# A transformer block conditioned by adaptive norms: the first block loaded and normalized in finer pieces, the last quarter's way through DRAM in two halves, and a new order

## The chip, the cores and the metric

The kernel runs on one NeuronCore of a Trainium2 chip. The core has five engines with their own instruction streams: TensorE (matrix products, PE in the profile, its weight loads PEld), VectorE (DVE), ScalarE (ACT), GpSimd (POOL) and SyncE (SP), whose stream here only issues transfers; some transfers are issued on ACT's stream. The metric is the device time of one execution in microseconds (us), median of several runs.

## The reference

All data are float32. `x` is [2, 2048, 512], `cond` [2, 512]; the weights are `ada_w` [512, 3072], two 512 x 512 matrices `ssm_w1`, `ssm_w2`, and `ff_w1` [512, 1024], `ff_w2` [1024, 512].

```python
emb = silu(t) @ ada_w + ada_b
shift_msa, scale_msa, gate_msa, shift_mlp, scale_mlp, gate_mlp = split(emb, 6)
norm = _ln(x) * (1.0 + scale_msa[:, None]) + shift_msa[:, None]
h = gelu(norm @ ssm_w1 + ssm_b1, approximate=False)
x = x + gate_msa[:, None] * (h @ ssm_w2 + ssm_b2)
norm2 = _ln(x) * (1.0 + scale_mlp[:, None]) + shift_mlp[:, None]
hf = gelu(norm2 @ ff_w1 + ff_b1, approximate=True)
x = x + gate_mlp[:, None] * (hf @ ff_w2 + ff_b2)
```

`_ln` subtracts the mean of a row and divides by the root of its variance plus 1e-6.

## The kernel before

The 4096 tokens are eight blocks of 512. A block lies with 128 partitions and four slots (`C = 4`): a partition holds four tokens of 512 features. Products of two matrices are done with seven smaller products instead of eight (`P1` to `P7`, on quarters and on sums of quarters of the operands); the sums are tensor_tensor instructions on VectorE or POOL (`tt`, line 345). In the feed-forward part this is done twice, so that a product has 49 leaves.

**Start.** `small_loads` brings the condition, `ada_b` and the biases as rows; TensorE turns them into columns (`turn_by_pe`, line 393) and VectorE copies them to `cols_t` (line 1405). `load_x(0, 2)` brings the first block in two pieces of two slots. `load_ada(g)` brings the sixth `g` of `ada_w`: 0 the shift, 1 the scale (in two pieces by rows). `w1` comes in two pieces by rows. Until the first data are there TensorE multiplies the identity with itself (`warm`). `normed_half(h)` takes statistics of slots 2h and 2h+1 (lines 613, 614), computes the root on POOL (646, 647) and the scale factors on VectorE (649 to 652), and normalizes one slot on VectorE (672) and one on ACT (363). `rows_of` multiplies silu(cond) with a sixth of `ada_w`, 32 columns of the array at a time; `modulation` then transposes the result in 32 x 32 pieces on VectorE (570), adds `ada_b` (573) and so makes `mods[g]`. `turn_in(h)` transposes the normalized half on TensorE, `turn_out(h)` scales and shifts it into `turned` (747 on VectorE, 363 on ACT). Then the products of the first block begin (`ssm1`, line 383), in the order P1, P2, P5 (`FRESH`): P1 and P2 take the first half of `w1`'s columns, P5 the sum of the two quarters of the second half, done on POOL.

**Middle.** The state-space part goes over the blocks, the feed-forward part over four pairs of blocks: `up` and `down`, whose leaves TensorE does one after the other while VectorE adds them up.

**End.** `down` of the last pair gives four quarters (two halves of the features for each of two blocks). Two of them go back to token order through DRAM (`quarter_out`): VectorE transposes in 32 x 32 pieces (1160), four transfers write `back_d`, others read it back, an add joins the rest `x1` (1177) and the result goes out. The other two are turned on TensorE (`turned_by_pe`): a scaled add (1136) of each leaf, two transposes, an add (1288), and the output.

**Order.** A class `Plan` collects all operations with a cost and with the operations that each depends on. `order` simulates the engines and puts the operations of each in a line; the list `MOVED` then takes single operations out and puts them behind a named one on a named engine ("v" VectorE, "a" ACT, "g" POOL, "s" SP), and `BEHIND` makes an operation wait for another. TensorE's operations stay in program order. The numbers in both lists count the operations in the order in which the program adds them. Transfers take turns at eight semaphores, so one is issued when the one eight before it has landed.

Of the kernel before, what the change touches and what calls it, by code (L numbers as in the profile page):

```python
# [58 lines left out]
)  # L59


# [226 lines left out]
def kernel(  # L288
# [21 lines left out]
    C = 4  # L310
# [1227 lines left out]
```

## Time and profile before

| what | value |
|---|---|
| median of 3 runs | 560.1 us (560.06 to 560.17) |
| profiled execution | 560.02 us, span 558.2 us |
| TensorE busy | 552.0 us (99% of the span), 2809 products |
| VectorE busy | 475.3 us (85%) |
| POOL busy | 384.0 us (69%) |
| ACT busy | 282.3 us (51%) |
| transfers | 123.68 MB, mean 222 GB/s |

The profile gives one execution. A row of a timeline has the start, the duration, the engine, the line, the operation with output and input tiles, how many instructions were merged, and in brackets how long the engine was idle before and what ended it. A float32 product shows as two records. Lines 345, 363, 372, 383, 393 and 405 are helpers that all stages use.

### The profile page before, as it was taken

The numbers are of one execution on the slowest core, as the hardware profiler recorded it, in microseconds if no ns is written. First come the engines' busy times: TensorE is split into PE (matmuls) and PEld (weight loads), VectorE is DVE, ScalarE is ACT, GpSimd is POOL, SyncE is SP. The second block draws the span as 40 slices with busy tenths as digits, with TensorE's granted clock in tenths as the row PEclk, the third lists the DMA queues.
The fourth block names the chain that finished last, engine by engine and source line by source line (L and its number), as shares of the span: only waits on it lengthen the run. The fifth ranks groups of instructions, "written<-read, shape, count | busy, mean of one in ns | idle before, by whom it ended". The sixth has DMA issues, their size and how long they took to land.

```text
span 558.2 us, 8726 instructions
## 1 busy us (share of the span) xinstructions
PE 552.0 (99%) x2809; PEld 482.0 (86%) x2809; DVE 475.3 (85%) x857; ACT 282.3 (51%) x523; POOL 384.0 (69%) x466
## 2 busy tenths in 40 slices
PE   8999999999999999999999999999999999999996
PEld 4888889899898988888888888888888888888885
DVE  5796878989778579799999987789988889898887
ACT  3473957675787845656305347414346414344230
POOL 2788639988855279985766868676757777539762
PEclk9999999999999999999999999999999999999999
DMA  8964699988399987995101999711998712983426
GB/s 311 399 234 115 193 354 275 360 260 267 113 292 323 290 318 231 329 300 188 40 37 38 285 305 323 229 39 42 293 322 286 234 39 59 326 285 112 153 76 188
DMA packets 66945, 123.68 MB, mean 222 GB/s; under 512 B 5668, under 2 KB 34260, under 8 KB 65364
## 3 DMA queue, kind: packets, MB, share of 16 engines
q1 hardware_dynamic: 64880, 121.80, 66.4%
q10 hardware_dynamic: 2020, 1.34, 0.8%
q8 instruction: 22, 0.36, 0.3%
q14 instruction: 23, 0.19, 0.1%
HBM read 77.89 MB, written 44.18 MB: 219 GB/s over the span
## 4 chain that ended last, share of the span: by engine, by line
PE 97%; DMA 2%; DVE 1%; DVEq 0%; issue 0%
PE bank L383 96%; DMA fw<-in_L_cond_ada_w_dram 1%; PE bank L393 1%; DMA fw<-in_L_cond_ada_b_dram 0%; DVE hidden L345 0%; DVE near L345 0%; DVE turned L747 0%; DVE rows L1136 0%; DVE bank L570 0%; DVEq L1533 0%; DVE mod L573 0%
## 5 line engine op out<-in xcount | busy, mean ns | idle before, releaser
L383 PE MATMUL bank<-turned,ring 128*128 128x256 f32 x896 | 210.1, 380 | 0.2 <-DVE turned L747 0.2
L383 PEld LDWEIGHTS bank<-turned,ring 128*128 128x128 f32 x896 | 167.9, 190 | 23.0 <-ACT turned L363 0.5
L345 DVE TENSOR_TENSOR hidden<-bank,hidden 128x512 f32<-128x512 f32 (+2 forms) x178 | 126.6, 739 | 22.2 <-PE bank L383 19.6
L383 PE MATMUL bank<-near,hidden 128*128 128x256 f32 (+1 forms) x470 | 95.0, 349 | 0.0
L383 PEld LDWEIGHTS bank<-near,hidden 128*128 128x128 f32 x470 | 82.2, 190 | 9.1
L383 PE MATMUL bank<-far,fw 128*128 128x256 f32 (+1 forms) x354 | 85.8, 374 | 0.0
L345 POOL TENSOR_TENSOR turned<-turned 128x512 f32<-128x512 f32 (+1 forms) x58 | 66.7, 1162 | 24.7 <-DVE turned L345 10.8
L383 PE MATMUL bank<-ring 128*128 128x256 f32 x336 | 82.3, 379 | 0.0
L345 DVE TENSOR_TENSOR rows<-bank,rows 128x256 f32<-128x256 f32 (+1 forms) x142 | 66.0, 479 | 15.4 <-PE bank L383 13.4
L383 PEld LDWEIGHTS bank<-far,fw 128*128 128x128 f32 x354 | 66.6, 190 | 8.7
L383 PEld LDWEIGHTS bank<-ring 128*128 128x128 f32 x336 | 63.7, 190 | 9.0 <-issue 0.3
L372 ACT COPY bank<-bank 128x512 f32<-128x512 f32 (+2 forms) x84 | 37.8, 449 | 62.5 <-PE bank L383 59.1
L363 ACT ACTIVATE hidden<-hidden,cols 128x512 f32<-128x512 f32 (+1 forms) x66 | 44.9, 710 | 42.0 <-DVE hidden L345 41.9
L345 POOL TENSOR_TENSOR hidden<-hidden 128x128 f32<-128x128 f32 (+2 forms) x44 | 45.0, 1033 | 26.0 <-DVE hidden L345 10.8
L383 PE MATMUL bank<-near,fw 128*128 128x256 f32 (+1 forms) x246 | 60.6, 376 | 0.0
L383 PE MATMUL bank<-hidden,fw 128*128 128x256 f32 (+1 forms) x216 | 53.3, 376 | 0.0
L383 PEld LDWEIGHTS bank<-near,fw 128*128 128x128 f32 x246 | 46.4, 190 | 6.1
L363 ACT ACTIVATE turned<-turned,mod,mod 128x512 f32<-128x512 f32 x56 | 42.3, 806 | 10.3 <-DMA turned<-turned 10.3
L383 PEld LDWEIGHTS bank<-hidden,fw 128*128 128x128 f32 x216 | 40.3, 190 | 5.9 <-issue 0.4
L345 POOL TENSOR_TENSOR ring<-turned,ring 128x256 f32<-128x256 f32 x41 | 29.6, 733 | 22.0 <-PE bank L383 19.0
L363 ACT ACTIVATE rows<-rows,gb,mod 128x512 f32<-128x512 f32 (+1 forms) x34 | 26.3, 787 | 33.2 <-DVE rows L345 21.3
L345 POOL TENSOR_TENSOR fw<-fw 128x256 f32<-128x256 f32 (+1 forms) x36 | 34.5, 968 | 7.0 <-DVE far L345 2.6
(123 smaller groups left out, 736.2 us busy)
## 6 DMA issues: line engine op xcount, KB each, us to landing
ring<-fw_parts SPq DMA_DIRECT2D x28, 512.0 KB
turned<-far SPq DMA_DIRECT2D x52, 256.0 KB
ring<-fw_parts SPq DMA_DIRECT2D x28, 384.0 KB
turned<-turned SPq DMA_DIRECT2D x32, 256.0 KB
back<-far SPq DMA_DIRECT2D x52, 128.0 KB
rows<-back SPq DMA_DIRECT2D x13, 512.0 KB
fw_parts<-fw SPq DMA_DIRECT2D x21, 256.0 KB
fw<-in_L_cond_ada_w_dram SPq DMA_DIRECT2D x5, 1024.0 KB
```

Of the source, the lines that this page charges most:

```text
L345: lambda E: E.tensor_tensor(o, a, b, f),
L363: lambda E: E.activation(o, a, func, bias=bias, scale=scale),
L372: plan.add("a", lambda E: E.copy(o, a), [o], [a], {"a": cost}, {"a": cost + 60})
L383: lambda E: E.matmul(o, lhsT, rhs, start=start, stop=stop, skip_group_check=True, **kw),
L393: lambda E: E.matmul(o, a, identity, start=start, stop=stop, is_transpose=True, skip_group_check=True),
```

## The change

- A row of ones and `ada_b`'s scale part (`one_more`) and a tile of ones (`two`) are set; `begin_rows` adds scale bias plus one to the scale's rows as the first TensorE product of their accumulation. The transposed rows are then used in place (`scale_t`), and VectorE adds nothing for g = 1. Two `warm` products behind the turn of the small rows fall away.
- The first block is loaded as slot 0, slot 1, slots 2 and 3; the scale's sixth in pieces of two, one and one row blocks; `w1` in two pieces by columns.
- TensorE does `turn_in(0)` ahead of both `rows_of`, slot by slot.
- The last quarter through DRAM (`by_half`) is written, read back, added and put out in two halves of its features. The first such quarter's adds are all on VectorE in the last pair.
- The last leaf (P4) of the last quarter is scaled, added and put out in two pieces.
- `MOVED` has 239 entries instead of 158, `BEHIND` 66 instead of 86; all entries are new. Among them: `(2, "a", 21)` puts the load of `ada_b`'s rows behind the first Silu on ACT, `(0, "g", -1)` and `(20, "g", 0)` put the memsets of `one_more` and `two` first on POOL, `(45, "v", 41)` puts the copy of the small columns behind the third of the four small VectorE steps, `(131, "s", 13)` and `(132, "s", 131)` put two loads of the gate's bias behind the scale's second piece, `(47, "a", 120)` puts an early Gelu (which loads its table) behind `turn_out(1)`.

```diff
+    one_more, two = kb(hidden_r, 30, 2)[:2], kb(hidden_r, 29, 1)[:2, P : P + G]
+    scale_t = kept("scale", P)
+    mods[1] = cut(scale_t, "p (n q) -> p n q", n=KD)[:, :, :B]
...
-    def rows_of(g, bank, midway=lambda: None):
+    def rows_of(g, bank, begun=False):
...
-            if k == KD // 2:
-                midway()
             for m in range(M):
-                mm(pa[m * G : (m + 1) * G, :P], silu[:, k, :], w[:, k, m], k == 0, k == KD - 1, (0, m * G))
+                mm(pa[m * G : (m + 1) * G, :P], silu[:, k, :], w[:, k, m], k == 0 and not begun, k == KD - 1, (0, m * G))
...
+    def begin_rows(bank):
+        for m in range(M):
+            o, row = banks[bank][m * G : (m + 1) * G, :P], cut(one_more, "p (n m q) -> p m n q", n=KD, q=G)[:, m]
+            mm(o, two, row, True, False, (0, m * G))
+
+    def modulation(g, bank, begun=False):
+        pa = rows_of(g, bank, begun)
+        o, a = scale_t if begun else pa[:, P : 2 * P], pa[:, :P]
         plan.add("v", lambda E: E.transpose(o, a), [o], [a], {"v": 210}, {"v": 290})
+        if begun:
+            return
...
+        closing = s + 1 == NBLK // 2
+        by_half = closing and blk == 1
+        band = cut(bands[n], "p (e a c r) -> p e c a r" if by_half else "p (a c e r) -> p e c a r", a=M, c=C, e=2)
...
+            if by_half:
+                half = kb(bands[n], 2 * e, 2)
+                for f in range(M):
+                    dma(halves[e, :, :, f].rearrange("a q r -> q a r"), cut(half[f * G : (f + 1) * G], "p (a r) -> p a r", a=M), queue(f) if e else "s")
+                dma(kb(flat, 2 * e, 2), halves[e].rearrange("a q f r -> (a q) (f r)"))
+        x, to = rest_in(s, d, blk, rest[n])
+        if by_half:
+            for e in range(2):
...
+                tt("vg", o, a, o, ALU.add)
+                dma(to[:, :, c], x[:, :, c], "s")
...
-                scaled_add(r1, t, columns(s, 1, e, 0)[1])
+                step = P if f == "P4" else HT
+                for c in range(0, HT, step):
+                    scaled_add(r1[:, c : c + step], t[:, c : c + step], columns(s, 1, e, 0)[1])
...
-            tt("v", x, bank[:, :, e], x, ALU.add)
-            dma(got["out"][:, c, d], x, "sa"[e])
+            step = 1 if blk == 0 and f == "P4" else 2
+            for n in range(0, 2, step):
+                c, d = slice(2 * h + n, 2 * h + n + step), slice(e * P, (e + 1) * P)
+                x = got["x"][:, c, d]
+                tt("v", x, bank[:, n : n + step, e], x, ALU.add)
+                dma(got["out"][:, c, d], x, "sa"[(e + n) % 2])
...
+    memset(one_more, 1.0)
     small_loads()
+    dma(one_more[:1], ada_b[D : 2 * D].unsqueeze(0), "a")
...
-    load_x(0, 2)
+    load_x(0, (1, 1, 2))
     load_ada(0)
-    load_ada(1, 2)
-    for k in range(0, KD, 2):
-        dma(w1_t[:, k : k + 2], w1[k * P : (k + 2) * P, :].rearrange("(k p) n -> p k n", p=P))
+    load_ada(1, (2, 1, 1))
+    for h in range(2):
+        c = slice(h * D // 2, (h + 1) * D // 2)
+        dma(w1_t[:, :, c], w1[:, c].rearrange("(k p) n -> p k n", p=P))
...
-    warm((6,), C)
-    warm((7,), 1)
+    begin_rows(2)
...
+    normed_half(1)
+    turn_in(0)
     modulation(0, 1)
-    modulation(1, 2, lambda: turn_in(0))
+    modulation(1, 2, True)
     turn_out(0)
-    normed_half(1)
```

More of the change, by code (lines that the diff above doesn't have):

```diff
@@ L493 @@
     half_t, zero = small_t[:, :C], small_t[:, C:]
-    marks = [kept(f"marks_{n}", 60) for n in range(4)]
+    marks = [kept(f"marks_{n}", 56) for n in range(4)]
     R_COND, R_ADA = 0, B * KD
@@ L534, with load_x, load_ada @@
     CARRIED = ("P1", "P5", "P6", "P2", "P7", "P3", "P4")
-    def load_x(i, pieces=1, xs=xs):
-        for s in range(pieces):
-            c = slice(s * C // pieces, (s + 1) * C // pieces)
-            dma(xs[i][:, c], x_blk[i][:, c], sooner=1000.0 * (pieces - 1))
-    def load_ada(g, pieces=1):
-        n = KD // pieces
-        for k in range(0, KD, n):
+    def load_x(i, pieces=(C,), xs=xs):
+        at = 0
+        for n in pieces:
+            c = slice(at, at + n)
+            dma(xs[i][:, c], x_blk[i][:, c], sooner=1000.0 * (len(pieces) > 1))
+            at += n
+    def load_ada(g, pieces=(KD,)):
+        k = 0
+        for n in pieces:
             dma(ada_t[g][:, k : k + n], ada_w[k * P : (k + n) * P, g * D : (g + 1) * D].rearrange("(k p) n -> p k n", p=P))
+            k += n
     def load_w(t, w, lead=0.0):
@@ L1156, in quarter_out @@
             act(done[:, e], done[:, e], AF.Identity, *columns(s, d, e, blk))
-        band = cut(bands[n], "p (a c e r) -> p e c a r", a=M, c=C, e=2)
+        closing = s + 1 == NBLK // 2
+        by_half = closing and blk == 1
+        band = cut(bands[n], "p (e a c r) -> p e c a r" if by_half else "p (a c e r) -> p e c a r", a=M, c=C, e=2)
+        queue = lambda f: "sa"[f % 2] if closing else "s"
+        far_t = back_d[s][d][blk]
+        flat = done.rearrange("p e t -> p (e t)")
+        halves = far_t.rearrange("p f r -> (p f r)").rearrange("(e a q f r) -> e a q f r", e=2, a=M, q=G, f=M)
         for e in range(2):
@@ L1160, in quarter_out @@
             plan.add("v", lambda E, o=o, a=a: E.transpose(o, a), [o], [a], {"v": 636}, {"v": 705})
-        closing = s + 1 == NBLK // 2
-        queue = lambda f: "sa"[f % 2] if closing else "s"
-        far_t = back_d[s][d][blk]
+            if by_half:
[6 more added lines that the diff above has]
+            for e in range(2):
+                c = slice(e * P, (e + 1) * P)
+                o = cut(x[:, :, c], "p c (f r) -> p c f r", f=M)
+                a = cut(kb(flat, 2 * e, 2), "p (f c r) -> p c f r", f=M, c=C)
+                tt("vg", o, a, o, ALU.add)
+                dma(to[:, :, c], x[:, :, c], "s")
+                plan.closing.append((plan.ops[-1].n, -1000.0))
+            quarters[0] += 1
+            return
         for f in range(M):
             dma(far_t[:, f].rearrange("(a q) r -> q a r", a=M), cut(bands[n][f * G : (f + 1) * G], "p (a r) -> p a r", a=M), queue(f))
-        flat = done.rearrange("p e t -> p (e t)")
-        by_slots = lambda t, h: cut(t, "p (f h r) -> p h f r", f=M, h=2)[:, h]
-        for h in range(2 if closing and blk else 0):
-            dma(by_slots(flat, h), far_t.rearrange("p f (h r) -> p h f r", h=2)[:, h])
-        if not closing or not blk:
-            dma(flat, far_t.rearrange("p f r -> p (f r)"))
-        x, to = rest_in(s, d, blk, rest[n])
+        dma(flat, far_t.rearrange("p f r -> p (f r)"))
         for h in range(2):
@@ L1176, in quarter_out @@
             a = cut(flat, "p (f c e r) -> p c e f r", f=M, c=C, e=2)[:, c].rearrange("p c e f r -> p (c e) f r")
-            tt("v" if closing and not blk else "vg", o, a, o, ALU.add)
+            tt("v" if closing else "vg", o, a, o, ALU.add)
             if closing:
-                dma(to[:, c], x[:, c], "s" if blk else queue(h))
-                plan.closing.append((plan.ops[-1].n, -1000.0 if blk else -4000.0))
+                dma(to[:, c], x[:, c], queue(h))
+                plan.closing.append((plan.ops[-1].n, -4000.0))
         if not closing:
@@ L1362 @@
     memset(silu, 0.0)
+    memset(two, 1.0)
     act(marks[0][:, 52:56], half_t, AF.Silu)
@@ L1394, in room, with turn_in @@
         return banks[bank][:, part * W : (part + 1) * W]
-    def turn_in(h):
-        for k in range(KD):
-            turn_rows_in(xn, k, room(h, k), range(2 * h, 2 * h + 2), (k != 3, k != 2))
+    def turn_in(h, sides=(0, 1)):
+        for c in sides:
+            for k in range(KD):
+                at = room(h, k)[:, c * P : (c + 1) * P]
+                turn_by_pe(at, xn[:, 2 * h + c, k * P : (k + 1) * P], ident, c == 0 and k != 3, c == 1 and k != 2)
     def turn_out(h):
@@ L1410 @@
     )
-    act(marks[0][:, 56:60], silu[:, 0, :4], AF.Gelu)
+    act(marks[1][:, 52:56], silu[:, 0, :4], AF.Gelu)
     plan.ops[-1].cost["a"] += 1300.0
-    for g in (1, 4):
+    for g in (4,):
         rows_g = cols_t[:, R_ADA + g * KD : R_ADA + (g + 1) * KD]
@@ L1417 @@
     plan.add("v", lambda E: E.tensor_copy(picks, pick), [picks], [ident], {"v": 560}, {"v": 640})
+    plan.stage = "rows 1"
+    normed_half(1)
+    turn_in(0)
     modulation(0, 1)
-    modulation(1, 2, lambda: turn_in(0))
+    modulation(1, 2, True)
     turn_out(0)
-    normed_half(1)
     w1q = {"11": w1_t[:, :2, : D // 2], "12": w1_t[:, 2:, : D // 2], "21": w1_t[:, :2, D // 2 :], "22": w1_t[:, 2:, D // 2 :]}
```

9 lines of the change are left out of this document (2 added, 7 removed), and 87 rows, old and new, of tables (BEHIND, MOVED).

## The prediction, made before the change was run

> **What bounds the kernel now.** I read the table of engines first, then stretches of the run, then the chain of waits, then both ends in order of time. The table puts TensorE at the head of all engines; the row is one 500 us stretch (after its length: busy time and instructions of PE, PEld, DVE, ACT, POOL, then granted clock, DMA share, GB/s).
> ```profile
> 34.00:534.00 500.00, 500.00 (x2496) 441.66 (x2495) 431.21 (x758) 258.94 (x483) 354.99 (x427) 1.00 0.67 216
> ```
> TensorE is busy in all of the 500 us, at full clock. The change leaves the products there as they are, so the middle can be lost but not gained. What can be gained lies ahead of the first big product and behind the last one. The chain of waits (start, us, what) shows the first end:
> ```profile
> 12.87 0.34 DVE bank L570
> 13.21 0.02 issue
> 13.23 0.18 DVE mod L573
> 13.41 0.03 issue
> 13.43 0.55 DVE turned L747
> ```
> VectorE transposes the scale's rows, adds the bias and scales the first turned tile; the stream of products follows at 14.03. TensorE's own order until then:
> ```profile
> 1.34 6.41 PE L383 MATMUL bank<-far 128*128 128x512 f32 x8 [1.34 <-POOL far masks.py:199]
> 7.68 0.26 PE L393 MATMUL bank<-far,fw 48*128 48x48 f32 x1
> 7.87 1.35 PE L383 MATMUL bank<-far 128*128 128x512 f32 x4
> 9.23 1.08 PE L383 MATMUL bank<-fw,far 128*32 128x128 f32 x32
> 10.55 0.64 PE L383 MATMUL bank<-fw,far 128*32 128x128 f32 x16 [0.24 <-DMA fw<-in_L_cond_ada_w_dram]
> 11.13 1.09 PE L393 MATMUL bank<-far 128*128 128x128 f32 x8
> 12.15 0.64 PE L383 MATMUL bank<-fw,far 128*32 128x128 f32 x16
> 12.73 1.09 PE L393 MATMUL bank<-far 128*128 128x128 f32 x8
> 14.03 5.45 PE L383 MATMUL bank<-turned,ring 128*128 128x256 f32 x24 [0.21 <-DVE turned L747]
> ```
> Warm-up, the turn of the small rows, two more warm-ups, the shift's rows, half of the scale's, eight transposes, the other half, eight transposes. The other engines, the queues of SP and ACT (SPq, ACTq) and SP's waits, one line each from several answers:
> ```profile
> 2.06 0.32 ACTq L405 DMA_DIRECT2D fw<-in_L_cond_ssm_b_dram  x1
> 4.04 0.20 ACT L363 ACTIVATE marks<-small 128x4 f32<-128x4 f32 x1
> 4.84 0.69 DVE L613 BATCH_NORM_STATS2 marks<-far 128x6 f32<-128x512 f32 x1 [2.91 <-DMA far<-in_x_dram]
> 5.24 1.03 SPq L405 DMA_DIRECT2D ring<-in_L_cond_ssm_w_dram  x2
> 6.91 0.73 POOL L647 TENSOR_TENSOR marks<-marks,small 128x2 f32<-128x2 f32 x1
> 7.16 0.37 SPq L405 DMA_DIRECT2D fw<-in_L_cond_ada_w_dram  x1
> SPq L405 <- DMA fw<-in_L_cond_ssm_b_dram: 0.9, 1, 0.9
> 9.74 0.55 DVE L672 TENSOR_SCALAR far<-far,marks 128x512 f32<-128x512 f32 x1
> 13.22 0.40 SPq L405 DMA_DIRECT2D near<-in_L_cond_ssm_w_dram  x1
> SPq L405 <- DMA ring<-in_L_cond_ssm_w_dram: 2.1, 2, 1.1
> 14.70 2.95 POOL L345 TENSOR_TENSOR ring<-ring 128x512 f32<-128x512 f32 x2 [4.37 <-DMA ring<-in_L_cond_ssm_w_dram]
> 14.00:34.00 20.00, 19.97 (x126) 17.36 (x127) 17.18 (x32) 12.27 (x24) 15.86 (x18) 1.00 1.04 400
> ```
> SP waits there for earlier transfers to land before it may issue: at 13.22 for w1's first half, so that half landed about 13.2; POOL got the second at 14.70. The transfers run full (share 1.04, 400 GB/s), so what is loaded cannot come sooner, only be cut otherwise. The other end, and the drain in half-microsecond stretches:
> ```profile
> 541.19 0.70 DVE L1160 STREAM_TRANSPOSE far<-rows 128x512 f32<-128x512 f32 x1
> 543.52 0.70 DVE L1160 STREAM_TRANSPOSE far<-rows 128x512 f32<-128x512 f32 x1
> 547.92 1.22 SPq L405 DMA_DIRECT2D rows<-back  x2
> 551.60 1.27 POOL L345 TENSOR_TENSOR near<-rows,near 128x512 f32<-128x512 f32 x1 [4.71 <-DMA rows<-back]
> 553.38 1.08 DVE L345 TENSOR_TENSOR hidden<-bank,hidden 128x256 f32<-128x256 f32 x3
> 554.37 0.68 DVE L345 TENSOR_TENSOR near<-rows,near 128x512 f32<-128x512 f32 x1
> 554.48 0.38 ACTq L405 DMA_DIRECT2D out_dram<-hidden  x1
> 555.08 0.37 SPq L405 DMA_DIRECT2D out_dram<-near  x1
> 553.00:553.50 0.50, 0.42 (x4) 0.18 (x2) 0.50 (x2) 0.00 (x0) 0.00 (x0) 1.00 0.97 275
> 556.00:556.50 0.50, 0.00 (x0) 0.00 (x0) 0.00 (x0) 0.00 (x0) 0.00 (x0) 0.88 1.05 329
> 556.50:557.00 0.50, 0.00 (x0) 0.00 (x0) 0.00 (x0) 0.00 (x0) 0.00 (x0) 0.50 0.89 299
> ```
> TensorE's part is over by 554, but the transfers run full from 553 to 557: 275 GB/s, later 300. The last 256 KB wait for VectorE's add that ends at 555.05. The span closes at 558.2. The profiled execution took 560.02, 1.82 outside its span, and stands 0.08 below the median of 560.1.
>
> **The start, part by part.** *Order on TensorE.* The first eight transposes go ahead of both rows stages, so none stands behind the last weight piece. The work between the normalized tokens and the scale's rows stays: 1.03 of transposes, 1.08 and 1.26 of rows. Today it runs from 9.23 to 12.84 with 0.24 idle. With tokens ready by 8.3 the rows would end at 12.2, as the weights landed only shortly before 12.15; with tokens ready at 9.1, which I take, at 12.5.
>
> *x by slots.* Half the bytes come first (256 KB at 400 GB/s is 0.65), so the statistics start about 4.2 instead of 4.84; two take 1.6, POOL's two steps 1.0, four small VectorE steps 0.7, the normalization 0.55: 8.1, if nothing intervenes. But the copy of the turned small rows now stands in front of the last of these steps, and it waits for TensorE's turn of them (7.68 now; the warm-up waits for the identity, and two memsets on POOL are put ahead of it, some 0.4 by the plan's own cost, an estimate). So some 9.1 again, against 9.74 now for the normalization's start alone.
>
> *Bias by TensorE.* Four tiny products (32 records took 1.08, so eight take 0.27) replace 1.35 of warm-up, while TensorE waits anyway. The addition leaves the chain: 13.23 to 13.43, 0.20. The transpose stays at 0.34 (it writes to SBUF now instead of PSUM; the 512-column ones in the rows 541.19 and 543.52 do so at 0.70, no dearer by column), the scaling at 0.55. With rows at 12.5: 12.5 + 0.34 + 0.05 + 0.55 + 0.05 = 13.5 for the first product. TensorE's own eight transposes (1.09) end at 13.6, of which the last serve the third product; w1's first half is there at 13.2. Gain 0.5. Upper end 0.83, where w1 bars; lower end -0.7, which is the first rival. I take the value nearer the upper end, since every link but the small rows has its own row here.
>
> *w1 by columns, scale in three.* Same bytes; the half by columns serves the first two products whole, and the third's sum, 1.5 on POOL, still starts at 14.70 and ends by 16.2; the third product, two times 1.8 behind 13.5, needs it at 17.1. So nothing gained, and 0.9 of slack. One load more for x and one for the scale cost SP two issues of 0.4; two of the gate's tiny bias loads move between the scale's pieces. SP runs ahead of the pipe by over 5 us (w1 issued by 6.3, landed 13.2), so they are covered; were that cover gone, 1.5 us would fall on the scale.
>
> *ada_b's rows behind the Silu.* This load, first on ACT's queue now, is issued after 4.24, and the turn of all small rows waits for it. One issued at 2.06 delayed SP until 7.16: 5.1 us. I take under 4, since it brings more rows but fewer loads stand ahead; both ends are in the range.
>
> **The end.** *The DRAM quarter in halves.* The first half can be written from 541.89 instead of 544.22, and the second starts where it does now. Writes of 64 KB instead of 128, four more issues of 0.4 on SP and ACT, one more wait on SP between write and read-back: what stands behind it on SP are outputs of the other quarters, which have two queues. Both halves are back by 551.6, when the first is now; the adds take 0.68 or 1.27, so the last output of this quarter leaves by 552.9 instead of 555.08. If VectorE takes an add among its leaves, TensorE's turns wait up to 0.68.
>
> *P4 in pieces.* Two scalings and two adds for one each. An add of 512 columns took 0.68, one of 256 took 0.36 (a third of 1.08), so the fixed part is small: some 0.1 more per pair, 0.2 in all, for outputs of 64 KB. The last output leaves at 554.48 + 0.2 = 554.7 instead of 555.08, and its bytes take 0.22 instead of 0.87. End of transfers: 557.0 - 0.38 - 0.65 = 555.97; I take 0.9, since the others still drain at 275 to 300. Ends: 0.3 (only the 0.38, less an issue) and 1.25.
>
> *Finer packets.* This quarter's outputs become 512-byte runs instead of 1 KB. The 553.00 stretch holds outputs of 512-byte runs at 275 GB/s, the last one 1 KB runs at 299. For 512 KB that is 0.15 more, within the 0.9. The Trainium skill (DMA: Bandwidth & Descriptors, Specifications) calls 512 bytes or more enough for line rate. By that the finer runs cost nothing and the end gains 1.05. The trace speaks for the small price: 275 beside 400 GB/s for the loads.
>
> **The new order.** The two lists move 239 instructions instead of 158, and tie 66 behind another one instead of 86. In the middle the sum takes nothing for it: the 500 us row has no idle time to give back. Its lower end is a loss, priced as a rival.
>
> Sum: 0.5 + 0.9 = 1.4, so 560.02 - 1.4 = 558.6 by the profiled execution, 558.7 by the median.
>
> **The rivals.** *Late bias rows.* If the load issued at 4.25 takes 5.1 us again, the turn stands at 9.4 instead of 7.68. Copy 0.2, last small step 0.16, normalization 0.55: tokens at 10.4, rows end at 13.8, first product at 14.7. The start loses 0.7, the end gains 0.9: 559.9, no change. For it speaks the 5.1; against it that the queue has fewer loads ahead.
>
> *The end does not move.* If the outputs still fill the pipe to 556.7, 0.3 remains there: 559.3, no change. For it: 97 to 105% busy share. Against it: half a megabyte goes earlier.
>
> *VectorE in the feed-forward part (slower).* One stretch there, and TensorE's last two turns for the rival after it:
> ```profile
> 294.00:314.00 20.00, 20.00 (x94) 17.60 (x94) 20.00 (x38) 10.17 (x16) 13.13 (x16) 1.00 0.41 121
> 553.51 0.44 PE L393 MATMUL bank<-far,rows 128*128 128x128 f32 x2
> ```
> Here VectorE has no idle time either. Each sum that the new lists turn to it, and that POOL had, delays the leaves behind it by 0.68 and TensorE with them. Two undo the gain, four (2.7) make 561.4: slower. Against it: several of the new entries put sums on POOL, which has 7 of 20 free there.
>
> *The clock.* TensorE's last instruction ends at 553.95, and the granted clock falls within 556.00 to 556.50: 2.1 to 2.6 idle were enough. Without the two warm-ups it stands between 8 and 9.1, about 1 us. The price of a closed clock is half of what runs until it opens, up to 3.2 (half of the 6.41 of TensorE's first row): 3.2 more than 558.7 is 561.9: slower. Against it: 1 us is under half of 2.1. The Trainium skill (TensorE: Matmul & The Clock Gate, Part 1) puts it at an idle window of some 3.4 us, longer than the 2.1 to 2.6 seen here; by that the clock stays open all the more.
>
> **How the numbers follow.** Both ends gain: 0.58, 557.7 to 559.0, of which 0.55 faster. One of them alone (late rows 0.18, full pipe 0.10): 0.28, 559.2 to 560.1, no change but for 0.04. Slower, by VectorE 0.10 or the clock 0.02: 561 to 562. Something more gained than I see: 0.02. A measurement of this kernel tells 0.2%, 1.1 us. Faster 0.61, same 0.27, slower 0.12. The range of 557.7 to 560.1 leaves out these 0.12 and some 0.04 below.
>
> **What would show it.** First big product at 13.3 to 13.8, its releaser VectorE's scaling without an addition ahead; the turn of the small rows no later than 8.5; TensorE at 500 of 500 us in the middle; the last output some 1.7 before the span's end instead of 3.1, transfers over by 555.6. Wrong if the small rows are turned after 9, if the middle shows idle time, or if the transfers still run full until the end at 557.

## The result and the profile after

The change made the kernel slower: 565.19 us, median of five runs (563.72 to 566.91), against 560.17 for the kernel before, run beside it five times; ratio 1.0088 [1.0064, 1.0111]. The forecast was 558.7. The profiled execution of after is the slowest of the five, 566.91 with a span of 565.1; that of before took 560.02 with 558.2. Of the 6.9 between these two spans 6.0 lie ahead of the first big product. TensorE's order at the start, after:

```profile
1.85 5.21 PE L394 MATMUL bank<-far 128*128 128x512 f32 x8 [1.85 <-POOL small L421]
12.52 0.31 PE L404 MATMUL bank<-far,fw 48*128 48x48 f32 x1 [5.46 <-DMA fw<-in_L_cond_ff_b_dram]
12.76 0.65 PE L394 MATMUL bank<-hidden 2*32 2x128 f32 x8
13.78 1.97 PE L404 MATMUL bank<-far 128*128 128x128 f32 x8 [0.37 <-DVE far L694]
15.68 3.34 PE L394 MATMUL bank<-fw,far 128*32 128x128 f32 x64
...
20.05 4.15 PE L394 MATMUL bank<-turned,ring 128*128 128x256 f32 x18
```

The order is the one forecast, but the turn of the small rows stands at 12.52 (before: 7.68), behind 5.46 idle, and the first big product at 20.05 (before: 14.03). ACT's queue, and two of VectorE's rows of the same execution:

```profile
3.26 0.21 ACT L374 ACTIVATE marks<-small 128x4 f32<-128x4 f32 x1
5.19 0.30 ACTq L416 DMA_DIRECT2D fw<-in_L_cond_ada_b_dram  x1
6.75 0.26 ACTq L416 DMA_DIRECT2D fw<-in_L_cond_ssm_b_dram  x1
9.54 0.28 ACTq L416 DMA_DIRECT2D fw<-in_L_cond_ff_b_dram  x1
5.19 0.69 DVE L635 BATCH_NORM_STATS2 marks<-far 128x6 f32<-128x512 f32 x1 [0.37 <-DMA far<-in_x_dram]
6.75 0.69 DVE L635 BATCH_NORM_STATS2 marks<-far 128x6 f32<-128x512 f32 x1 [0.65 <-DMA far<-in_x_dram]
```

Not one load stands behind the Silu of 3.26 but three, and each is issued in the moment in which a large load of SP's queue lands: at 5.19 slot 1 of `x`, at 6.75 slots 2 and 3 (VectorE's statistics start on them in the same hundredth), at 9.54 the shift's sixth of `ada_w`, 1 MB. The chain of waits shows the last two (it follows `ada_w` to 9.52 and `ff_b` to 12.38):

```profile
2.11 7.41 DMA fw<-in_L_cond_ada_w_dram
...
9.54 2.83 DMA fw<-in_L_cond_ff_b_dram
```

Stretches of after, columns as before (the last but two is the granted clock):

```profile
11.00:13.00 2.00, 0.48 (x9) 0.38 (x9) 0.14 (x2) 0.00 (x0) 0.00 (x0) 0.69 0.47 113
15.00:17.00 2.00, 2.00 (x32) 1.57 (x34) 0.00 (x0) 0.23 (x1) 0.89 (x1) 0.50 0.95 308
34.00:534.00 500.00, 498.72 (x2494) 440.50 (x2493) 435.15 (x745) 263.24 (x490) 369.94 (x443) 1.00 0.67 218
```

The clock fell to half while TensorE had nothing: eight transposes took 1.97 (1.09 before) and 64 row records 3.34. In the middle TensorE is idle for 1.3. So the 6.9 are 6.0 at the start and 0.9 behind it; the latter are the 1.3 of the middle less 0.4.

### The profile page after: what moved, and what is told of

Its sections match the earlier page's. It is cut to its first block, busy times and chain, and to the rows that moved or that the text cites. A ratio compares the mean times of both kernels' runs of the same rounds, so it can differ in the third digit from the quotient of the medians.

```text
span 565.1 us, 8782 instructions
## 1 busy us (share of the span) xinstructions
PE 552.1 (98%) x2813; PEld 483.5 (86%) x2813; DVE 477.6 (85%) x839; ACT 281.8 (50%) x523; POOL 402.1 (71%) x486
## 4 chain that ended last, share of the span: by engine, by line
PE 96%; DMA 2%; DVE 1%; SPq 0%; issue 0%; DVEq 0%
PE bank L394 95%; DMA fw<-in_L_cond_ada_w_dram 1%; PE bank L404 1%; DVE hidden L356 1%; DMA fw<-in_L_cond_ff_b_dram 1%; SPq L416 0%; DVE far L694 0%; DVE cols L1449 0%; DVEq L1579 0%; DVE marks L674 0%
## 5 line engine op out<-in xcount | busy, mean ns | idle before, releaser
L356 DVE TENSOR_TENSOR hidden<-bank,hidden 128x512 f32<-128x512 f32 (+3 forms) x179 | 126.9, 737 | 26.0 <-PE bank L394 23.2
L356 DVE TENSOR_TENSOR rows<-bank,rows 128x256 f32<-128x256 f32 (+1 forms) x142 | 66.0, 481 | 14.1 <-PE bank L394 12.4
L356 POOL TENSOR_TENSOR hidden<-hidden 128x128 f32<-128x128 f32 (+2 forms) x45 | 45.3, 1016 | 22.5 <-DVE hidden L356 12.5
L356 POOL TENSOR_TENSOR fw<-fw 128x256 f32<-128x256 f32 (+1 forms) x42 | 42.0, 1013 | 7.1 <-DVE fw L356 6.9
L356 POOL TENSOR_TENSOR ring<-turned,ring 128x256 f32<-128x256 f32 x42 | 31.4, 758 | 16.3 <-PE bank L394 13.3
L356 POOL TENSOR_TENSOR far<-hidden,far 128x512 f32<-128x512 f32 x22 | 30.2, 1375 | 8.3 <-DVE near L356 3.1
```

Source lines behind the costliest of these rows:

```text
L356: lambda E: E.tensor_tensor(o, a, b, f),
```

## Experiments

"First" is the start of the first big product, "rest" the span less that, both of the profiled execution. For before they are 14.03 and 544.2, and the median beside each call was 560.0 to 560.2.

| kernel | first | rest | median (range; runs) | ratio to before |
|---|---|---|---|---|
| after | 20.05 | 545.1 | 565.19 (563.72-566.91; 5) | 1.0088 [1.0064, 1.0111] |
| e1 | 14.40 | 543.5 | 559.49 (559.09-562.45; 10) | 0.9999 [0.9987, 1.0012] |
| e2 | 17.05 | 543.5 | 564.02 (562.48-567.82; 5) | 1.0082 [1.0046, 1.0118] |
| e3 | 16.70 | 543.5 | 562.48 (560.75-564.21; 8) | 1.0047 [1.0033, 1.0062] |
| e4 | 19.21 | 543.5 | 564.54 (563.99-564.82; 4) | 1.0078 [1.0063, 1.0093] |
| e5 | 16.73 | 543.5 | 562.18 (560.60-563.70; 6) | 1.0039 [1.0026, 1.0053] |
| e6 | 18.16 | 543.6 | 562.84 (561.34-564.03; 6) | 1.0047 [1.0034, 1.0060] |
| e7 | 16.66 | 543.7 | 562.15 (561.89-564.02; 5) | 1.0043 [1.0031, 1.0055] |
| e8 | 17.98 | 543.1 | 561.46 (560.02-562.90; 6) | 1.0022 [1.0011, 1.0034] |
| e9 | 13.44 | 543.7 | 559.15 (558.87-561.12; 11) | 0.9980 [0.9961, 0.9999] |
| e10 | 14.05 | 545.1 | 559.90 (559.57-561.04; 11) | 0.9998 [0.9989, 1.0008] |
| e11 | 13.86 | 543.5 | 559.06 (558.86-560.34; 11) | 0.9985 [0.9976, 0.9994] |
| e12 | 14.07 | 544.0 | 559.90 (559.87-560.40; 11) | 0.9997 [0.9988, 1.0006] |
| e13 | 14.87 | 543.4 | 559.74 (559.66-560.08; 11) | 0.9993 [0.9984, 1.0002] |
| e15 | 14.06 | 543.7 | 559.52 (559.16-560.56; 11) | 0.9992 [0.9983, 1.0001] |
| e16 | 13.54 | 543.8 | 559.19 (558.90-559.81; 11) | 0.9986 [0.9977, 0.9994] |
| e17 | 15.30 | 544.2 | 561.48 (561.14-562.67; 6) | 1.0031 [1.0020, 1.0043] |

**The six small loads first on ACT's queue (e1).**

```diff
-(2,"a",21)
+(2,"a",-1),(5,"a",2),(1,"a",5),(3,"a",1),(4,"a",3),(6,"a",4)
```

> The changed kernel with one edit: the five loads of small rows (ada_b, ff_b, cond, ssm_b, ff_b) stand first on ScalarE's queue, the one load of the bias row sixth, and the Silu with its table load behind them. Theory (three small loads each stood behind a large transfer that held their completion semaphore): no small load waits for a large one, the turn of the small rows comes by 8.5 us instead of 12.52, TensorE's clock stays open, the first big product comes at 13.3 to 13.8 us instead of 20.05, and the time falls by 5 to 6 us, to about 559.5 (559 to 560.5). Rival A (the pieces of w1, by columns, and the first block's finer pieces land later by themselves): the small rows come early, but the first product stays later than 15.5 us and the time over 561.5. Rival B (the new order as a whole is slower in the middle): the first product comes early and the time stays over 562.

The median falls by 5.7 to 559.49, and first comes at 14.40 instead of 20.05: what the change lost at the start hangs on where these loads stand. (The ratio is near 1 because three of the ten runs took 561.0 to 562.5.) The start is later than the 13.3 to 13.8 expected and still not better than before. TensorE and SP's queue of e1, and one stretch:

```profile
7.18 0.26 PE L404 MATMUL bank<-far,fw 48*128 48x48 f32 x1
10.15 1.09 PE L404 MATMUL bank<-far 128*128 128x128 f32 x8 [2.36 <-DVE far L694]
14.40 0.89 PE L394 MATMUL bank<-turned,ring 128*128 128x256 f32 x3 [0.16 <-DMA ring<-in_L_cond_ssm_w_dram]
4.36 1.45 SPq L416 DMA_DIRECT2D fw<-in_L_cond_ada_w_dram  x3
4.00:7.00 3.00, 3.00 (x6) 0.97 (x5) 1.75 (x4) 0.56 (x2) 0.47 (x2) 1.00 0.86 299
```

The turn is on time (7.18). But with six loads on ACT's queue and three on SP's for `x`, `ada_w` is the one that must wait: issued at 4.36, when VectorE's statistics show slot 0 landed (4.37). The pipe has less to do from 4 to 7 (299 GB/s), and all that follows in it is late, up to `w1`, which releases the first big product.

**The clock kept open (e2).** `warm` does four products of the identity at the start; the last of them is issued five times.

```diff
 warm((0, 3, 4, 6), C)
+once = plan.ops[-1].fn
+plan.ops[-1].fn = lambda E: [once(E) for _ in range(5)][-1]
```

> The changed kernel with TensorE kept busy while it waits for the small rows: the last of the four products that are there only to warm it is issued five times (1.3 us each, from 7.06 to about 12.3 us). The loads are as late as before. Theory (of the 6.0 us that the first product is late, about 1.9 are a clock that fell during 5.46 us without work, 4.1 the late rows): the turn of the small rows stays at about 12.5, its 8 transposes behind it take 1.1 us instead of 1.97 and the 64 records of the rows 2.4 instead of 3.34, the first product comes at about 18.2, and the time falls by 1.5 to 2, to about 563.4. Rival (the slow records come from something else, for example from operands that land late): they stay at 1.97 and 3.34 and the time stays at 565.

TensorE's rows of e2's profiled execution:

```profile
11.88 0.23 PE L404 MATMUL bank<-far,fw 48*128 48x48 f32 x1 [0.29 <-DMA fw<-in_L_cond_ff_b_dram]
13.06 1.09 PE L404 MATMUL bank<-far 128*128 128x128 f32 x8 [0.60 <-DVE far L694]
14.08 1.95 PE L394 MATMUL bank<-fw,far 128*32 128x128 f32 x64
17.05 1.13 PE L394 MATMUL bank<-turned,ring 128*128 128x256 f32 x4
```

The small rows are nearly as late as in after (11.88 against 12.52), but from the turn to the first product it takes 5.17 instead of 7.53: about 2.4 of after's 6.0 are the closed clock, the other 3.6 the late rows. By time alone it can't be told: e2's five runs spread over 5.3. The span and the mean granted clock of each run help: three of e2's runs had spans of 560.5 to 561.0 at 0.998 to 1.000, two had 564.8 and 565.7 at 0.995 and 0.997; after's five had 0.992 to 0.997. So the longer warm-up did not hold the clock in every run. The span of 565.7 is longer than any of after's, whose run at 0.997 had 561.9; what else that run lost is not known.

**The same order with two semaphores (e3, e4).** `ada_b`'s load stands last of the small ones behind the Silu in both; the place of one load of the gate's bias on SP differs, and by it the load whose semaphore `ada_b`'s inherits.

```diff
+(3,"a",-1),(4,"a",3)       both, ahead of (2,"a",21)
-(131,"s",13)
+(131,"s",14)               e3: waits for a small load of ff_b
-(132,"s",131)
+(132,"s",14)               e4: waits for the load of cond
```

> The changed kernel with ssm_b's and ff_b's small rows first on ScalarE's queue, ada_b's still behind the Silu, and both small gate_b loads on SyncE's queue behind the last piece of the first weight. So ada_b's load takes a completion semaphore that a small load (ff_b) had before it. Theory (semaphores held by large transfers): ada_b's load is issued right behind the Silu at 3.3 to 3.6 us, lands by 6.5 to 7.5, the first product comes at 13.4 to 14.2 and the time is 559 to 560.5. Rival (a load behind the Silu is late as such, since its bytes queue behind the large ones): ada_b's rows land at 9 or later, as in the twin kernel, and the first product comes at 15 or later.

> As the kernel before it, but with one of the two gate_b loads ahead of the last piece of the first weight. The only difference that matters is which completion semaphore ada_b's load takes: here that of the load of x's slots 2 and 3. Theory: ada_b's load is issued only when that transfer has landed, at about 6.7 us, and lands at 9.3 to 9.7; the small rows are turned by 9.8, and the first product comes 5.6 us behind that, at 15.2 to 16.3, with the time at 561 to 562.5. Rival (semaphores don't matter): within 0.3 us of its twin in the first product and in the time.

ACT's queue, the load that the chain of waits names ahead of it, and TensorE, e3 and then e4:

```profile
1.65 3.28 DMA fw<-in_L_cond_ff_b_dram
4.95 0.30 ACTq L416 DMA_DIRECT2D fw<-in_L_cond_ada_b_dram  x1
10.04 0.23 PE L404 MATMUL bank<-far,fw 48*128 48x48 f32 x1 [1.65 <-DMA fw<-in_L_cond_ada_b_dram]
```

```profile
1.99 4.78 DMA fw<-in_cond_dram
6.78 0.30 ACTq L416 DMA_DIRECT2D fw<-in_L_cond_ada_b_dram  x1
11.68 0.31 PE L404 MATMUL bank<-far,fw 48*128 48x48 f32 x1 [3.33 <-DMA fw<-in_L_cond_ada_b_dram]
```

`ada_b`'s load is issued 0.02 after the load whose semaphore it inherits has landed: at 4.95 behind `ff_b`'s (landed 4.93), at 6.78 behind `cond`'s (landed 6.77). The inherited semaphore shifts the issue by 1.83, the first product by 2.5 (with the clock) and the median by 2.1. That is the theory's wait, shown. But the expectation of e4 had the wrong holder: it is not the load of slots 2 and 3 of `x` but one of 4 KB, which took 4.78 to land. So this pair does not show that the holder must be large; that large ones held the three loads of after rests on the times and the chain of after. The expectation that a free turn would bring e3 down to about 14 failed as well: a small load behind the large ones takes 5.1 from issue to use, and the clock closed in e3 too (the eight transposes took 1.97, the 64 records of the rows 2.56, in e2 1.09 and 1.95), which makes 1.5 of its 16.70.

**Only the bias row behind the Silu (e5).** 2 KB instead of `ada_b`'s 12 KB.

```diff
-(2,"a",-1),(5,"a",2),(1,"a",5),(3,"a",1),(4,"a",3),(6,"a",4)      (e1)
+(2,"a",-1),(5,"a",2),(1,"a",5),(3,"a",1),(4,"a",3),(6,"a",21)
```

> The changed kernel with the five loads of small rows first on ScalarE's queue and the bias row's load behind the Silu. Against the first experiment only that load has moved, and by it the first weight's load on SyncE's queue waits for the landing of ada_b's small rows (3.2 us) instead of that of x's first slot (4.3 us). Theory (large loads too are held by the semaphores of others): it is issued at 3.0 to 3.3 instead of 4.36, the transfers no longer stand at 280 to 330 GB/s between 4 and 7 us, w1's first half lands 0.5 to 0.9 earlier than at 14.26, the first product comes at 13.5 to 13.9, and the undisturbed runs take 558.6 to 559.1, 0.2% or more under the kernel before. Rival (w1's runs of 1 KB, which moved at 350 GB/s, are the whole of it): first product at 14.2 or later, time as in the first experiment, 559.1 to 559.8.

```profile
6.59 0.23 ACTq L416 DMA_DIRECT2D hidden<-in_L_cond_ada_b_dram  x1
10.77 0.42 PE L394 MATMUL bank<-hidden 2*32 2x128 f32 x8 [1.95 <-DMA hidden<-in_L_cond_ada_b_dram]
```

As the theory said, `ada_w` is issued earlier (2.62 instead of 4.36). But the bias row now waits for the semaphore of `ssm_b`'s rows (landed 6.57) and, issued at 6.59, is used at 10.77: 4.2 for 2 KB. The new products of the bias then hold TensorE, and first stands at 16.73. One row moved turned 14.40 into 16.73; some 1.6 of it are the clock again (transposes 1.67, rows 2.99).

**The middle of before under e5's start (e6), and one pair of sums ordered (e7).** e6 puts the instructions of the middle in the order of the kernel before (115 sums change engine); e7 makes one POOL sum wait for a VectorE sum.

```diff
 e6: e5 with the middle's lines from before
 e7: e5 with BEHIND +(1324, 1312)
```

> The kernel of the experiment before it, with its start and its last instructions (the last DRAM quarter in halves, P4 in pieces), but with the whole middle in the order of the kernel before: the lines of VectorE, ScalarE, GpSimd and SyncE are given in full, with 115 sums back on the other one of VectorE and GpSimd. Theory (the new order of the middle makes runs uneven, by sums of VectorE and GpSimd that collide; it gains nothing otherwise): the runs lie within 0.6 us of each other, and the median is that of the undisturbed runs of its twin, 558.6 to 559.3. Rival A (the unevenness is in the start): a spread of 2 us or more stays. Rival B (the new order itself brings the early end): median 559.6 or more.

> As e5_first_eight, but one sum of GpSimd (fw, 128x256, planned at 247.7 us) waits until VectorE's sum of fw (128x512) is done. In the profile of the changed kernel that VectorE sum took 2.90 us instead of 0.98 to 1.00, with two sums of GpSimd beside it, and TensorE stood still for 1.3 us. Theory (this one collision makes the slow runs): no run is more than 0.6 above the fastest, median 558.6 to 559.1. Rival (there are other places like it, or the slow runs come from elsewhere): some 3 of 10 runs stay 1.5 to 3 us above the fastest.

Neither decides anything: they spread over 2.7 and 2.1, e5 over 3.1, and with this late start the mean granted clock differs from run to run (0.992 to 1.000). The question was put again with a quiet start (e10, e15, e16).

**Less to drain (e8).** e5 with one instruction of the output changed; the kernel leaves out most of that part of the output.

```diff
-dma(to[:, :, c], x[:, :, c], "s")
+dma(to[:1, :, c], x[:1, :, c], "s")
```

> As e5_first_eight, with the two last outputs of the DRAM quarter cut to one partition of 128: 508 KB fewer are written in the last 6 us (that part of the output is left out). Theory (the end is held by the transfers, which run full at 275 to 296 GB/s from 553 to 556.5; the second output of 256 KB falls into that time): the last transfer ends 0.6 to 0.9 earlier and the time falls by 0.5 to 0.8 against its twin. Rival (the end is held by VectorE's last add and its own output): less than 0.2.

The rest falls by about 0.4, from 543.5 to 543.1, between the two expectations. Two stretches say why it is not more:

```profile
558.10:558.35 0.25, 0.00 (x0) 0.00 (x0) 0.24 (x1) 0.00 (x0) 0.00 (x0) 1.00 0.00 0
558.35:559.60 1.25, 0.00 (x0) 0.00 (x0) 0.00 (x0) 0.00 (x0) 0.00 (x0) 1.00 0.96 274
```

With 508 KB less the pipe runs empty (0 GB/s) just ahead of the last outputs, and then needs 1.25 full for those alone. What is issued last is a bound of its own, and only about 0.4 below the drain's.

**x in two pieces again (e9).**

```diff
 e1 with  -load_x(0,(1,1,2))
          +load_x(0,(2,2))
```

> The changed kernel with the six small loads first on ScalarE's queue and x in two pieces again, as before the change. With one large load fewer, the bias row's load gets a completion semaphore that nobody held, and the first weight's load waits for ada_b's small rows (3.2 us) instead of x's first slot (4.3 us). All lines of the order are given in full; a tiny memset keeps the numbering. Theory (the start is lost by loads that wait for others' semaphores, not by the bias product, the scale in three or w1's columns): small rows and bias row are there by 7.5, TensorE's clock stays at 1.00, the first product comes at 13.8 to 14.3, and the time is 559.2 to 559.8, with a spread under 1 us. Rival (finer pieces are not the cause): first product at 15 or later, 560.5 or more.

```profile
2.75 0.26 ACTq L440 DMA_DIRECT2D hidden<-in_L_cond_ada_b_dram  x1
2.74 2.85 SPq L440 DMA_DIRECT2D fw<-in_L_cond_ada_w_dram  x3
6.94 0.26 PE L428 MATMUL bank<-far,fw 48*128 48x48 f32 x1
9.08 1.09 PE L428 MATMUL bank<-far 128*128 128x128 f32 x8 [1.53 <-DVE far L718]
13.44 1.75 PE L418 MATMUL bank<-turned,ring 128*128 128x256 f32 x7
6.95 6.35 DMA ring<-in_L_cond_ssm_w_dram
```

One load less, one semaphore free: the first load of `ada_w` goes at 2.74 instead of 4.36, the tokens are transposed at 9.08 instead of 10.15, the first product starts at 13.44. It is the start that was forecast (13.5), without the piece of it that was to bring it about. The last row, of the chain of waits, has `w1`'s first half, landed at 13.30, as the last releaser; the forecast had VectorE's scaling there. The spread under 1 us did not come: two of the eleven runs took 560.7 and 561.1.

**w1 by rows again (e11), and the first half's steps ahead of the second half's statistics (e13).**

```diff
 e11: e9 with w1 in two pieces by rows
 e13: e9 with the statistics of slots 2 and 3 (50 to 53) behind 43
```

> As e9_x_in_two, with w1 in two halves by rows again (runs of 2 KB instead of 1 KB). In the twin the first product (13.44) was released by w1's first half by columns (landed 13.30). Theory (two sides: runs of 2 KB move at 400 instead of 350 GB/s, 0.3 us over the 1 MB, but the first products then need both halves): the second half lands at 13.6 to 13.9, first product at 13.7 to 14.0, time 0.2 to 0.5 above the twin, so the cut by columns is worth that. Rival (the cut by columns costs by its short runs): first product at 13.3 or earlier, time at or under the twin's.

> As e9_x_in_two, with one more edit: on VectorE the statistics of slots 2 and 3 (4 instructions) stand behind the steps that normalize slots 0 and 1, not ahead of them. In the first experiment VectorE stood there for 1.01 us, waiting for x's second half. Theory (this wait, which the new order brought, holds the tokens): tokens are ready 0.8 to 1.3 us earlier than in its twin, then the last piece of the scale's weights (landed 11.9 to 12.7 us) bounds the rows; first product 0.2 to 0.5 earlier, time 558.8 to 559.4. Rival (the weights bound the rows anyway): first product and time within 0.15 of the twin.

e11, by rows: from 13 to 14 the pipe carries 404 GB/s, in e9, by columns, 363. First came at 13.86 instead of 13.44, and yet the median is 559.06 against 559.15: no difference, where 0.2 to 0.5 was expected. e13 missed both expectations: the tokens are transposed at 9.46 (9.08 in e9) and the first product comes at 14.87.

```profile
12.11 0.16 DVE L695 TENSOR_TENSOR marks<-marks 128x2 f32<-128x2 f32 x1 [1.10 <-POOL marks L693]
13.80 0.30 DVE L614 STREAM_TRANSPOSE scale<-bank 128x128 f32<-128x128 f32 x1
```

The second half's small steps now wait 1.10 for POOL and, in VectorE's fixed order, the scale's transpose stands behind them (12.34 in e9, 13.80 here). A stall was moved, not removed.

**The old start under the new middle and end (e10).**

```diff
 after with the loads, rows and normalization of the first block as before
```

> The kernel before, its start untouched (loads, small rows, modulation, first tiles), with the changed kernel's order of the middle and its end (last DRAM quarter in halves, P4 in pieces): the start alone is undone. Theory (all of the loss is in the start; from the first product to the end of the span the new form takes 543.5 us where the kernel before takes 544.2): first product at 14.0, span 557.5, time 559.4 (559.2 to 559.7), all runs within 0.6 us. Rival (the new order of the middle is uneven by itself): stalls of 1 us or more in some runs, spread over 1.5 us, median 560 or more.

First is 14.05, as in before, and the median 559.90: all of the 5 us was the start. The wait in the middle is there again. VectorE, POOL and the list of waits of e10, and then the same of after:

```profile
242.97 2.67 DVE L379 TENSOR_TENSOR fw<-fw 128x512 f32<-128x512 f32 x1
243.12 1.98 POOL L379 TENSOR_TENSOR fw<-fw 128x256 f32<-128x256 f32 x2
PE bank L417 <- DVE hidden L379: 1.1, 1, 1.1
```

```profile
248.91 2.90 DVE L356 TENSOR_TENSOR fw<-fw 128x512 f32<-128x512 f32 x1
249.30 1.96 POOL L356 TENSOR_TENSOR fw<-fw 128x256 f32<-128x256 f32 x2
PE bank L394 <- DVE hidden L356: 1.3, 1, 1.3
```

One VectorE sum takes 2.67 and 2.90 instead of the 0.7 to 1.0 of the other executions, beside two POOL sums of 1.96 to 1.98 together, and the leaves behind it are late. Four of e10's eleven runs took 560.65 to 561.04, the other seven at most 560.04: it happens in some executions only.

**The pair ordered under e9's start (e16), and the middle of before under it (e15).**

```diff
 e16: e9 with BEHIND +(1324, 1312)
 e15: e9 with the middle's lines from before
```

> As e9_x_in_two (first product at 13.44), with GpSimd's sum of fw (128x256) waiting until VectorE's sum of fw (128x512) beside it is done. Theory (this collision makes the runs at 560.7 and 561.1, 3 of 11 or so): all runs within 0.5 us of each other, median 558.9 to 559.2. Rival (other collisions of the new order, or the start): 2 or more of 11 runs stay 1 us or more above the fastest.

> As e9_x_in_two, with the middle in the order of the kernel before (VectorE, ScalarE, GpSimd, SyncE). Theory (the new order of the middle gives nothing and makes runs uneven): all runs within 0.5 us, median 558.8 to 559.3, under the kernel before by 0.15% or more. Rival (the new middle gives some of the gain): median 559.5 or more.

In e16 the VectorE sum takes its usual time and POOL follows:

```profile
242.62 0.74 DVE L380 TENSOR_TENSOR fw<-fw 128x512 f32<-128x512 f32 x1
243.44 3.20 POOL L380 TENSOR_TENSOR fw<-fw 128x256 f32<-128x256 f32 x3 [0.62 <-DVE fw L380]
```

None of its eleven runs is over 559.81 (median 559.19). With the pair unordered, 8 of 54 runs of e1, e9, e10, e11 and e13 have a span at least 0.6 longer than the others of their kernel, but all of them in e1 (3), e9 (1) and e10 (4): e11 and e13 have none either. So none of 11 in e16 says little. The collision is seen in the traces of after and e10; that it makes the other long runs is not shown. In e9's execution the same pair, unordered, went the other way: VectorE's sum took 0.73 and POOL's first 1.19 instead of 0.75. e15 gave 559.52, 0.33 more than e16, but with the same rest (543.7) and a later first product (14.06): a gain by the new middle itself is not shown.

**The new end alone (e12), and one load late alone (e17), both on the kernel before.**

```diff
 e12: before with the last quarter in halves, P4 in pieces, and their order
 e17: before with (1,"a",16): ada_b's load behind the Silu
```

> The kernel before with the end alone: last DRAM quarter in halves, P4 in pieces, and the order of the last instructions; start and middle as before the change. Theory (the 0.7 us come from the end, the order of the middle is worth 0.2 at most): 559.3 to 559.7. Rival (the gain belongs to the new order of the middle): 559.9 to 560.1.

> The kernel before with one edit: ada_b's load of small rows stands behind the Silu on ScalarE's queue. Its completion semaphore was held by x's first half, which has landed by then. Theory (one late load costs what the rival in the prediction said; the 6 us of the change come from three loads in a row, each held by a large transfer): issued at 4.3 to 4.9, landed at 8.3 to 9.4, first product at 14.2 to 14.9, time 560.2 to 561. Rival (the place behind the Silu alone makes it): first product at 16 or later, 562 or more.

e12, the stretches that the prediction showed of before:

```profile
553.00:556.00 3.00, 0.84 (x5) 0.29 (x3) 1.62 (x6) 0.00 (x0) 0.00 (x0) 1.00 1.00 285
556.00:556.50 0.50, 0.00 (x0) 0.00 (x0) 0.00 (x0) 0.00 (x0) 0.00 (x0) 1.00 0.95 284
556.50:557.00 0.50, 0.00 (x0) 0.00 (x0) 0.00 (x0) 0.00 (x0) 0.00 (x0) 1.00 0.12 33
```

The transfers end at about 556.6 instead of 557.0, but the span ends only 0.1 sooner (558.1), and the median falls by 0.18, with an interval of the ratio that includes no change. e17, ACT's queue and TensorE:

```profile
4.76 0.30 ACTq L405 DMA_DIRECT2D fw<-in_L_cond_ada_b_dram  x1
9.50 0.23 PE L393 MATMUL bank<-far,fw 48*128 48x48 f32 x1 [1.54 <-issue]
15.30 0.91 PE L383 MATMUL bank<-turned,ring 128*128 128x256 f32 x3 [0.21 <-DVE turned L747]
```

One late load alone, with its own semaphore wait and 4.7 from issue to use, costs 1.27 at the first product and 1.5 by medians, somewhat more than the expectation's 14.9 and 561. (Two of its six runs took 562.6, with a mean clock of 0.995, the other four 561.1 to 561.7.) The rival *Late bias rows* had 9.4 for the turn (9.50) and 14.7 for the first product (15.30).

## Why the prediction was wrong

**The step that failed: *ada_b's rows behind the Silu*.** It said "One issued at 2.06 delayed SP until 7.16: 5.1 us. I take under 4, since it brings more rows but fewer loads stand ahead". Two things were wrong in it. The size: 4.7 (e17), 5.1 (e3), so the 5.1 was nearer than the 4. And the count: it took one load to stand behind the Silu, and `ssm_b`'s and `ff_b`'s rows stand there too. The entry did not put them there: in e17 an entry of the same kind leaves both ahead of the Silu. Worked out from the code of after alone, not run, both stand behind it with or without the entry, and ahead of it once the bias row's load and the third piece of `x` are taken out. So the plan, which hands out the eight turns itself, put two small loads later because two loads were added; the prediction counted the added loads as issues on SP only. Three loads, each held until a large transfer of the other queue gave its semaphore free (5.19, 6.75, 9.54), end at 12.38, where one ends at 9.5. The eight turns stand in the description of the kernel, and the prediction's own rows show SP waiting for `ssm_b`'s load of ACT's queue; the step did not walk through the turns the other way. e1 shows the cost whole (5.7 by medians), e3 and e4 that an issue waits for the semaphore's earlier load.

***The clock*.** "2.1 to 2.6 idle were enough" was the bound, and 1 us idle the forecast; 5.46 came, and the clock closed, at a cost of 2.4 (bound: 3.2). It is a consequence of the late rows: with rows on time (e1, e9) it stayed open, with 2.36 idle in e1. The length that closes it is not fixed: e5 idled 1.95, did 0.4 of work, and its clock fell in the next two us; in e3 it fell behind 1.65 idle, 0.6 of work and 0.60 idle. The Trainium skill ("TensorE: Matmul & The Clock Gate", "Part 1: The HAM clock gate (the "warmup" mystery)") describes a free-running window of about 3.4 us; fixed windows agree better with these three than any one length of idleness, but no run here measured the window.

***x by slots*.** The load's half bytes were counted, its place among the eight was not: the third piece of `x` holds `ada_w` back by 1.6 (e1 against e9). "So some 9.1 again" came true in e9, at 9.08, with two pieces.

***Bias by TensorE*, *Order on TensorE*.** Right as links: in e9 the scale's rows are transposed at 12.34 (12.5 forecast) and the first product starts at 13.44 (13.5), with tiny products of 0.42 in all (0.27 forecast). That `w1`'s landing at 13.30 came last, and at nearly the same time, is luck for the number. *w1 by columns*: "So nothing gained" held by time (e11), though the pipe is slower by columns (363 against 404 GB/s), which had not been counted.

**The end: a term mis-sized.** 0.9 was taken; e12 has 0.18 by medians and 0.1 by span, not clear of noise. The last outputs leave as worked out (VectorE's last piece runs from 554.38 to 554.71 in e12; 554.7 was forecast). But the drain is still full at 285 until 556.5: the rival *The end does not move*, with 0.3. e8 shows a second floor about 0.4 below it, the last pieces' own bytes. What is still missing, 0.3 between the earlier end of transfers and the span's, no row explains.

***The new order*.** "In the middle the sum takes nothing for it" did not hold: in some executions 1.1 to 1.3 are lost where a VectorE sum meets POOL sums. The rival *VectorE in the feed-forward part* had a late leaf as its price too, but another mechanism, an added sum instead of a collision.

Two things stay open. Kernels with the new start and the new end have a rest of 543.4 to 543.8 where the middle lost nothing, with the old middle too (e6, e15); e12 has 544.0, and no wait shows the difference. And after minus e1 is 5.7 by medians, 5.65 by first product, while e2 splits this into clock and rows in one execution only.

The best versions are e16, e9 and e11, 559.1 to 559.2: 0.14 to 0.20% below before. Once the small loads go first and `x` stays in two pieces, the change is worth about 0.9 of the 1.4 forecast.

## What to carry to other kernels

When an instruction that issues a transfer is moved, list everything that its queue issues behind it, and for each the transfer whose semaphore it inherits: a few KB then wait for megabytes of another queue. Do the same when a load is added or split: it takes a turn even where it costs no bytes, and the order may push others back for it. Cutting the last output into finer pieces gains little while the pipe is full; look at the share of transfers until the end first. An order that never leaves the bottleneck idle on average can still lose time in some executions where two engines' sums meet, so look at several executions.

## What the runs showed of the hardware

- A small load issued among large ones took 3.3 to 4.8 us to land while these kept the transfers busy, with little regard to its size: 2 KB 3.3 (e3), 4.1 and 4.5 (e5), 4 KB 4.1 (e9) and 4.8 (e4), 12 KB 4.8 (e3, e4). In after, where they ran empty (82 GB/s from 11.0 to 12.4), 4 KB took 2.8.
- VectorE's sum of two SBUF tiles took 2.67 (e10) and 2.90 (after) instead of 0.7 to 1.0 where POOL did sums beside it. The Trainium skill ("SBUF — State Buffer", "SBUF: two separate sides") says that the two share a pair of ports which one holds for a whole instruction. The traces agree with such a wait: VectorE's sum ended 0.5 behind the second POOL sum in both (e10 245.64 and 245.10, after 251.81 and 251.26). That it lost to both sums, not one, and only in some executions, the page does not say.
- The granted clock that fell to 0.50 behind 5.46 us without work cost 2.4 at the start of the kernel (after against e2), more than the 1.35 of warm-up that the change took away there.
